# Output bias written by ScalarE under an accumulating gather of the residual, in a sparse graph-attention kernel

## The chip, the cores and the metric

The kernel runs on one core of a Trainium2 chip, in one launch. The metric is the device time of that launch in microseconds (us). Three runs of the kernel before gave 1980.19, 1983.63 and 1985.25 us; the median, 1983.63 us, is the time before. The profiled execution took 1980.11 us and its span, from the first to the last instruction, is 1978.3 us.

## The reference

A layer of graph attention with a residual and a layer norm, for x of 16 x 1024 x 512 and one 1024 x 1024 adjacency matrix of zeros and ones (few ones: a node has a handful of neighbours, a few nodes have many), all float32:

```python
q = (x @ Wq + bq).reshape(b, n, H, HD)      # H = 8 heads of HD = 64
k = (x @ Wk + bk).reshape(b, n, H, HD)
v = (x @ Wv + bv).reshape(b, n, H, HD)
scores = einsum('bqhd,bkhd->bhqk', q, k) / sqrt(HD)
scores = scores + (1.0 - adj)[None, None, :, :] * -1000000000.0
attn = softmax(scores, axis=-1)
out = einsum('bhqk,bkhd->bqhd', attn, v).reshape(b, n, d)
attn_out = out @ Wo + bo
x = _layernorm(x + attn_out, axis=-1)       # mean and variance over the 512, eps 1e-5
```

The change concerns the last two lines alone: the output product, its bias (`bo`), the residual x and the sum over the 512 columns that the layer norm starts from. The kernel folds the value bias through Wo into the output bias once, at the start (L345), so that `bo_bc`, a 128 x 512 tile, holds the whole bias, the same in every partition.

## The kernel before

**Tiling.** A batch is 1024 nodes, taken as 8 tiles of 128 queries. At the start the kernel counts the neighbours of each node, sorts the nodes by that count and writes lists of neighbours; `asked_row` holds, for each tile, the rows of its 128 queries in x. The attention of a tile is done in blocks, each with one neighbour per query: 35 blocks per batch, 560 in all. For a block, GpSimd gathers the key and value rows (`kvg`, L849), VectorE multiplies and sums (`qk` L870, `s` L874), ScalarE takes the exponential (L884) and weighs the value rows, eight small instructions per block (L894; for some blocks VectorE does it, L898), and VectorE adds up (L910); for the nodes with many neighbours TensorE adds up (`sum`, L919 and L920). `normalise` then divides (o, L939), TensorE transposes o (`poT`, L947) and ScalarE copies the transposed tile out of PSUM (`oT`, L951).

**Fronts.** The products of x with the query, key and value weights of all batches are a list of units, `fronts`, worked off between the blocks (L565 for the query, L679 for key and value, which are done by a scheme with fewer products and more additions). The last fronts are placed some blocks before the last batch begins.

**Finishing a tile.** `finish` (L760) makes the output product of a transposed tile (`po`, four matmuls of 128x512, L565) and plans what follows: `out` adds the product to the residual tile `y`, with the row sum as a by-product (`accum_out`), then `centre`, `spread` (ScalarE squares, L781), `variance`, `power` (GpSimd, L787), `shift`, `norm_out` (ScalarE, L793) and `store`, a scatter by GpSimd into the output (L797). The bias enters in one of two ways. While there are fronts left, VectorE makes two passes, `y = p + y` (L771) and `y = bo_bc + y` with the row sum (L772). When no fronts are left (`biased`), TensorE adds the bias by a fifth matmul of 128x512 in the middle of the output product (L814), and VectorE makes one pass (L772 with p in place of bo_bc).

**The residual tile.** `load_y` (L743) takes a buffer of the tag "y" (6 of them) and fills it ahead of the finishing: for the tiles 0 to 101 by an indirect gather of 128 rows of x (`gather_x`, L732, GpSimd), for the tiles 102 to 127 by a plain load by SyncE of a tile that was sorted at the start. That sorting is `sort_residual` (L738): two tiles a step over 13 steps of the start, each a gather into a "y" buffer and, two steps later, a store by SyncE to DRAM (`residual`). So the y gathers are 26 at the start and 102 in the course of the work. The tiles 102 to 111 also have their transposed attention output spilled to DRAM and reloaded when the fronts are done, so that the finishing of the last 22 tiles or so falls into the last stage.

**What sets the order.** The order on each engine is written out by the program: one pass of the main loop (L1045) is a step, about one block. Within a step come the exponentials of block n + 3, the products of n + 4, the gathers up to n + 8, the weighing, the sums, then what was planned for this step by `later(k, fn)` (k steps ahead), then `later_last`, then the loads of y for tiles that will be finished soon, and then units of TensorE (finishing first, fronts after) as far as a credit goes. `sort_residual` is called at the end of a step. Each engine works through its own list in that order, and waits on semaphores where it needs another engine or a transfer. A tile is finished two steps after its y was asked for at the earliest (`n > loaded + 1`), and its `out` comes a step after its last matmul.

Of the kernel before, what the change touches and what calls it, by code (L numbers as in the profile page):

```python
# [14 lines left out]
OP = mybir.AluOpType  # L15
# [33 lines left out]
PRODUCT = 0.86  # L49
# [6 lines left out]
P = 128  # L56
# [103 lines left out]
def kernel(  # L160
# [36 lines left out]
    nc = tc.nc  # L197
# [15 lines left out]
    ident = const.tile([P, P], F32, name="ident")  # L213
    make_identity(nc, ident)
    W = {}
# [3 lines left out]
    bo_bc = const.tile([P, D], F32, name="bo_bc")  # L219
# [8 lines left out]
    with ExitStack() as main:  # L228
# [6 lines left out]
        def fill_psum(name):  # L235
            return psum.tile([P, HALF], F32, tag="fill", name=name, bufs=4)
# [48 lines left out]
        residual = [dram.tile([P, D], F32, name=f"residual_{i}") for i in range(B * NT - SPILL[0])]  # L285
# [65 lines left out]
        def later(k, fn):  # L351
            plan.setdefault(now[0] + k, []).append(fn)

        def later_last(k, fn):
            rest.setdefault(now[0] + k, []).append(fn)
# [167 lines left out]
        X, XT, SX, KV, VSUM, NRM, Y, OT, PS = {}, {}, {}, {}, {}, {}, {}, {}, {}  # L523
# [35 lines left out]
        def product(name, lhs, w, out):  # L559

            def unit(c):
                if c == 0:
                    PS[name] = fill_psum(name)
                p = PS[name]
                nc.tensor.matmul(p, lhs()[:, ts(c, P)], w[:, c, :], start=(c == 0), stop=(c == NPAIR - 1))  # L565
                if c == NPAIR - 1:
                    del PS[name]
                    later(1, lambda: out(p))

            return [(PRODUCT, lambda c=c: unit(c), None) for c in range(NPAIR)]  # L570
# [159 lines left out]
        loaded = {}  # L730

        def gather_x(y, b, t):  # L732
            nc.gpsimd.indirect_dma_start(  # L733
                out=y, out_offset=None, in_=x_rows,
                in_offset=bass.IndirectOffsetOnAxis(ap=asked_row[:, t:t + 1], axis=0), element_offset=b * N * D,
            )

        def sort_residual(i):  # L738
            y = work.tile([P, D], F32, tag="y", name=f"y_sorted_{i}", bufs=Y_BUFS)
            gather_x(y, *divmod(SPILL[0] + i, NT))  # L740
            later(2, lambda: nc.sync.dma_start(residual[i], y))

        def load_y(b, t, k=None):  # L743
            if k is None:
                Y[b, t] = work.tile([P, D], F32, tag="y", name=f"y_{b}_{t}", bufs=Y_BUFS)
            else:
                Y[b, t] = work.tile([P, 2, D], F32, tag=f"t{k % 4 + 1}", name=f"y_{b}_{t}", bufs=1)[:, 0, :]
            loaded[b, t] = now[0]
            if b * NT + t >= SPILL[0]:
                nc.sync.dma_start(Y[b, t], residual[b * NT + t - SPILL[0]])  # L750
            else:
                gather_x(Y[b, t], b, t)
# [6 lines left out]

        def finish(b, t):  # L760


            biased = not fronts

            def out(p):
                OT.pop((b, t))
                y = Y[b, t]

                st = small.tile([P, 5], F32, name="stats", bufs=6)
                if not biased:  # L770
                    nc.vector.tensor_tensor(y, p, y, op=OP.add)  # L771
                nc.vector.scalar_tensor_tensor(  # L772
                    y, p if biased else bo_bc, 1.0, y, op0=OP.mult, op1=OP.add, accum_out=st[:, 0:1]
                )

                def centre():
                    nc.vector.tensor_scalar(st[:, 1:2], st[:, 0:1], -1.0 / D, None, op0=OP.mult)

                def spread():
                    sq = work.tile([P, D], F32, tag="ysq", name=f"ysq_{b}_{t}", bufs=1)  # L780
                    nc.scalar.activation(sq, y, AF.Square, bias=st[:, 1:2], accum_out=st[:, 2:3])  # L781

                def variance():
                    nc.vector.tensor_scalar(st[:, 2:3], st[:, 2:3], 1.0 / D, EPS, op0=OP.mult, op1=OP.add)  # L784

                def power():
                    nc.gpsimd.tensor_tensor(st[:, 3:4], st[:, 2:3], neg_half, op=OP.pow)  # L787

                def shift():
                    nc.vector.tensor_tensor(st[:, 4:5], st[:, 3:4], st[:, 1:2], op=OP.mult)  # L790

                def norm_out():
                    nc.scalar.activation(y, y, AF.Identity, bias=st[:, 4:5], scale=st[:, 3:4])  # L793
                    later(2, store)

                def store():
                    nc.gpsimd.indirect_dma_start(  # L797
                        out=out_rows[b, t], out_offset=bass.IndirectOffsetOnAxis(ap=asked_row[:, t:t + 1], axis=0),
                        in_=y, in_offset=None, element_offset=b * N * D,
                    )  # L800
                    del Y[b, t]

                later(1, centre)
                later_last(2, spread)
                later(3, variance)
                later(4, power)
                k = 5 if fronts else 6
                later(k, shift)
                later_last(k + 1, norm_out)

            units = product(f"po_{b}_{t}", lambda: OT[b, t], W["o"], out)
            if biased:
                def bias():
                    nc.tensor.matmul(  # L814
                        PS[f"po_{b}_{t}"], ident[:, 0:1].to_broadcast([P, P]), bo_bc, start=False, stop=False
                    )

                units.insert(2, (PRODUCT, bias, None))
            return units

# [198 lines left out]
        done, coming, spilled, gathered, fronts, guarded = [], [], [], [0], [], []  # L1021
# [9 lines left out]
        with tc.manual_schedule():  # L1031
# [13 lines left out]
            while n < total or plan or rest or urgent or done or finishing or spilled or not guarded:  # L1045
# [45 lines left out]
                while credit > 0 or urgent:  # L1091
                    if urgent and not (first_unit and fronts):
                        urgent.pop(0)()
                        continue
                    if (
                        not finishing and len(done) > (LAZY if fronts else 0) and n > loaded.get(done[0], n) + 1
                        and n > last_finish + 1 and not total - 2 <= n < total
                    ):
                        finishing = finish(*done.pop(0))
                        last_finish = n  # L1100
                    units = finishing or fronts
                    if not units:
                        if urgent:
                            urgent.pop(0)()
                            continue
                        break
                    cost, fn, ready = units[0]
                    if ready and not ready():
                        if urgent:
                            urgent.pop(0)()  # L1110
                            continue
                        break
                    del units[0]
                    fn()
                    credit -= cost
                    first_unit = False
# [3 lines left out]
                if n in SORTED_AT:  # L1120
                    for i in range(2):
                        sort_residual(2 * (n - SORTED_AT[0]) + i)
# [35 lines left out]
```

## Time and profile before

| | |
|---|---|
| time, median of three runs | 1983.63 us |
| span of the profile | 1978.3 us |
| granted TensorE clock, mean | 0.990 |
| moved by the DMA engines | 563.10 MB, 285 GB/s in the mean |
| of it by GpSimd's queue | 403.22 MB, 61.4% of 16 engines' time |
| of it by SyncE's queue | 153.16 MB, 20.9% |
| gathers of y (102 and 26), 256 KB each | median 5.1 and 6.4 us from issue to landing |
| gathers of key and value rows (560), 512 KB each | median 5.9 us |
| scatters of the output (128), 256 KB each | median 5.2 us |
| finished tiles with the bias on VectorE, on TensorE | 106, 22 |

How to read it: the span is one execution; the busy time of an engine is the time in which it had an instruction in work. A row of a group of instructions gives the line, the engine, the operation, the tiles (out<-in), the count, then the busy time in us and the mean in ns of one; after the bar stands how long the engine was idle just before such instructions, and what it waited for. TensorE's float32 matmul is recorded as two instructions, so 22 bias products stand there as x44. A mean duration overlaps with the next instruction's; where a cost is wanted, the distance from start to start in the time line is the better number.

### The profile page before, as it was taken

The numbers are of one execution on the slowest core, as the hardware profiler recorded it, in microseconds if no ns is written. First come the engines' busy times: TensorE is split into PE (matmuls) and PEld (weight loads), VectorE is DVE, ScalarE is ACT, GpSimd is POOL, SyncE is SP. The second block draws the span as 40 slices with busy tenths as digits, with TensorE's granted clock in tenths as the row PEclk, the third lists the DMA queues.
The fourth block names the chain that finished last, engine by engine and source line by source line (L and its number), as shares of the span: only waits on it lengthen the run. The fifth ranks groups of instructions, "written<-read, shape, count | busy, mean of one in ns | idle before, by whom it ended". The sixth has DMA issues, their size and how long they took to land. (4 is left out here: it accounts for less than half of the span.)

```text
span 1978.3 us, 25784 instructions
## 1 busy us (share of the span) xinstructions
PE 1913.1 (97%) x5379; PEld 925.0 (47%) x5379; DVE 1785.8 (90%) x3694; ACT 1566.4 (79%) x6152; POOL 1301.4 (66%) x1224
## 2 busy tenths in 40 slices
PE   7988999999999999999999999999999999899896
PEld 4434454444545454454545445454544545444443
DVE  3799999998999999999998999999899999999785
ACT  4526788888787888879887887979888798988895
POOL 1663566767667675767667686766767675566784
PEclk9999999999999999999999999999999999999898
DMA  6796887888889788888879788888978889988984
GB/s 252 219 366 244 263 303 247 301 284 279 303 272 323 262 305 270 303 287 286 304 260 319 257 301 277 295 304 267 315 254 288 285 311 311 321 308 287 317 290 143
DMA packets 191140, 563.10 MB, mean 285 GB/s; under 512 B 31711, under 2 KB 31739, under 8 KB 190974
## 3 DMA queue, kind: packets, MB, share of 16 engines
q0 software_dynamic: 121632, 403.22, 61.4%
q1 hardware_dynamic: 66736, 153.16, 20.9%
q10 hardware_dynamic: 2606, 4.99, 0.7%
q14 instruction: 122, 1.00, 0.2%
q8 instruction: 44, 0.72, 0.1%
HBM read 442.25 MB, written 143.71 MB: 296 GB/s over the span
## 5 line engine op out<-in xcount | busy, mean ns | idle before, releaser
L849 POOL DMA_INDIRECT kvg<-kv_rows,key_row x560 | 632.7, 1130 | 425.3 <-ACT pv L894 123.1
L894 ACT ACTIVATE pv<-kvg,pv 128x64 f32<-128x64 f32 x3608 | 908.7, 339 | 0.1
L565 PE MATMUL pq<-wq,xT 128*128 128x512 f32 x1024 | 477.4, 596 | 1.5 <-DVE q L595 0.9
L565 PE MATMUL po<-wo,oT 128*128 128x512 f32 x944 | 437.0, 595 | 4.7 <-DVE y L771 1.9
L874 DVE TENSOR_REDUCE s<-qk 128x8 f32<-128x512 f32 x560 | 381.1, 681 | 6.1
L870 DVE TENSOR_TENSOR qk<-qt,kvg 128x512 f32<-128x512 f32 x464 | 317.6, 684 | 3.6 <-DMA kvg<-kv_rows,key_row 3.6
L565 PEld LDWEIGHTS pq<-wq,xT 128*128 128x128 f32 x1024 | 191.4, 191 | 219.8 <-issue 201.6
L565 PEld LDWEIGHTS po<-wo,oT 128*128 128x128 f32 x944 | 175.4, 191 | 206.0 <-issue 189.4
L679 PE MATMUL pp<-t,s 128*128 128x512 f32 x504 | 237.2, 593 | 6.3 <-DVE s L551 6.3
L679 PE MATMUL x<-b,xT 128*128 128x512 f32 x504 | 237.1, 593 | 0.0
L910 DVE TENSOR_TENSOR pv<-pv,pv 128x520 f32<-128x520 f32 x336 | 233.3, 694 | 0.0
L884 ACT ACTIVATE pv<-s,absent 128x8 f32<-128x8 f32 x464 | 135.8, 293 | 105.8 <-DVE s L874 67.8
L797 POOL DMA_INDIRECT out_dram<-y,asked_row x128 | 152.4, 1190 | 38.9 <-issue 21.0
L833 POOL DMA_INDIRECT qt<-q_rows,asked_row x128 | 140.9, 1101 | 36.7 <-issue 33.1
L575 ACT ACTIVATE sq_k<-kv 128x128 f32<-128x128 f32 x512 | 150.7, 299 | 8.8 <-DVE kv L702 8.8
L679 PEld LDWEIGHTS pp<-t,s 128*128 128x128 f32 x504 | 94.7, 190 | 115.3 <-issue 103.4
L679 PEld LDWEIGHTS x<-b,xT 128*128 128x128 f32 x504 | 94.7, 190 | 112.2 <-issue 107.6
L733 POOL DMA_INDIRECT y<-in_x_dram,asked_row x102 | 117.2, 1149 | 30.6 <-issue 28.5
L843 POOL DMA_INDIRECT qg<-q_rows,query_row x96 | 105.9, 1103 | 26.8 <-issue 23.0
L679 PE MATMUL z<-t,s 128*128 128x512 f32 x252 | 120.2, 600 | 0.0
L679 PE MATMUL z<-b,s 128*128 128x512 f32 x252 | 118.6, 593 | 1.2 <-DVE kv L707 1.2
L679 PE MATMUL pp<-t,xT 128*128 128x512 f32 x252 | 118.4, 592 | 0.0
(185 smaller groups left out, 2625.7 us busy)
## 6 DMA issues: line engine op xcount, KB each, us to landing
kv_rows<-kv SPq DMA_DIRECT2D x128, 512.0 KB
x<-in_x_dram SPq DMA_DIRECT2D x128, 256.0 KB
q_rows<-q SPq DMA_DIRECT2D x128, 256.0 KB
kvg<-kv_rows,key_row POOLq DMA_INDIRECT x560, 5.9
residual<-y_sorted SPq DMA_DIRECT2D x26, 256.0 KB
y<-residual SPq DMA_DIRECT2D x26, 256.0 KB
adj<-in_adj_dram POOLq DMA_DIRECT2D x8, 512.0 KB, 10.9
spill<-oT SPq DMA_DIRECT2D x10, 256.0 KB
```

The lines of the kernel that those rows point to most:

```text
L565: nc.tensor.matmul(p, lhs()[:, ts(c, P)], w[:, c, :], start=(c == 0), stop=(c == NPAIR - 1))
L575: nc.scalar.activation(sq, s[:, ts(h, P)], AF.Square, scale=scale, accum_out=sums[:, h:h + 1])
L679: nc.tensor.matmul(R[bank], l[:, ts(c, P)], right[:, c, :], start=(first and c == 0), stop=(c == 1), skip_group_check=True,)
L733: nc.gpsimd.indirect_dma_start(out=y, out_offset=None, in_=x_rows, in_offset=bass.IndirectOffsetOnAxis(ap=asked_row[:, t:t + 1], axis=0), ...
L797: nc.gpsimd.indirect_dma_start(out=out_rows[b, t], out_offset=bass.IndirectOffsetOnAxis(ap=asked_row[:, t:t + 1], axis=0), in_=y, in_offse ...
L833: nc.gpsimd.indirect_dma_start(out=QT[b, t], out_offset=None, in_=q_rows[b % ROWS], in_offset=bass.IndirectOffsetOnAxis(ap=asked_row[:, t: ...
L849: nc.gpsimd.indirect_dma_start(out=KG[n], out_offset=None, in_=kv_rows[b % ROWS], in_offset=bass.IndirectOffsetOnAxis(ap=key_row[:, g:g + ...
L870: nc.vector.tensor_tensor(QK[n], q, KG[n][:, 0:D], op=OP.mult)
L874: nc.vector.tensor_reduce(S[n], QK.pop(n).rearrange("p (h d) -> p h d", d=HD), axis=AX.X, op=OP.add)
L884: nc.scalar.activation(PV[n][:, D:], S.pop(n), AF.Exp, bias=bias)
L894: nc.scalar.activation(pv[:, ts(h, HD)], v[:, ds(D + h * HD, HD)], AF.Copy, scale=pv[:, D + h:D + h + 1])
L910: nc.vector.tensor_tensor(PV[b, t], PV[b, t], pv, op=OP.add)
```

## The change

The bias is taken out of `finish` altogether. Before the gather of a y tile, ScalarE copies `bo_bc` into the tile, and one step later GpSimd gathers the rows of x with an addition (`compute_op=OP.add`), so that the DMA engines add x to the bias that is there. `y` then holds x + bias when it is used, VectorE needs one pass in every tile, and TensorE no bias matmul in any. In the sorting at the start the store to DRAM moves from two steps after the call to three, since the gather is issued one step later. The aim is to take the bias off VectorE and TensorE.

```diff
         def gather_x(y, b, t):
-            nc.gpsimd.indirect_dma_start(
+
+            nc.scalar.copy(y, bo_bc)
+            later(1, lambda: nc.gpsimd.indirect_dma_start(
                 out=y, out_offset=None, in_=x_rows,
                 in_offset=bass.IndirectOffsetOnAxis(ap=asked_row[:, t:t + 1], axis=0), element_offset=b * N * D,
-            )
+                compute_op=OP.add,
+            ))
 
         def sort_residual(i):
             y = work.tile([P, D], F32, tag="y", name=f"y_sorted_{i}", bufs=Y_BUFS)
             gather_x(y, *divmod(SPILL[0] + i, NT))
-            later(2, lambda: nc.sync.dma_start(residual[i], y))
+            later(3, lambda: nc.sync.dma_start(residual[i], y))
...
         def finish(b, t):
 
-
-            biased = not fronts
-
             def out(p):
                 OT.pop((b, t))
                 y = Y[b, t]
 
                 st = small.tile([P, 5], F32, name="stats", bufs=6)
-                if not biased:
-                    nc.vector.tensor_tensor(y, p, y, op=OP.add)
-                nc.vector.scalar_tensor_tensor(
-                    y, p if biased else bo_bc, 1.0, y, op0=OP.mult, op1=OP.add, accum_out=st[:, 0:1]
-                )
+                nc.vector.scalar_tensor_tensor(y, p, 1.0, y, op0=OP.mult, op1=OP.add, accum_out=st[:, 0:1])
...
-            units = product(f"po_{b}_{t}", lambda: OT[b, t], W["o"], out)
-            if biased:
-                def bias():
-                    nc.tensor.matmul(
-                        PS[f"po_{b}_{t}"], ident[:, 0:1].to_broadcast([P, P]), bo_bc, start=False, stop=False
-                    )
-
-                units.insert(2, (PRODUCT, bias, None))
-            return units
+            return product(f"po_{b}_{t}", lambda: OT[b, t], W["o"], out)
```

## The prediction

> **What bounds the kernel now.** First the page's line of busy times, for the engine that is nearest to full. Then the busy times by stretch, because the kernel has stages: columns are the stretch, its length, the busy us (and instructions) of TensorE's matmuls, weight loads, VectorE, ScalarE and GpSimd, the granted clock, the DMA engines' share and GB/s. The first row below is the start, in which the 26 residual tiles are sorted; the others are the bulk and the end.
>
> ```profile
> PE 1913.1 (97%) x5379; PEld 925.0 (47%) x5379; DVE 1785.8 (90%) x3694; ACT 1566.4 (79%) x6152; POOL 1301.4 (66%) x1224
> ```
>
> ```profile
> 75.00:155.00 80.00, 71.53 (x183) 31.61 (x182) 72.96 (x139) 22.71 (x91) 51.35 (x48) 1.00 0.95 344
> 210.00:1650.00 1440.00, 1436.04 (x4067) 696.74 (x4066) 1345.10 (x2753) 1194.30 (x4756) 998.10 (x918) 1.00 0.85 288
> 1770.00:1831.00 61.00, 59.11 (x157) 27.69 (x158) 56.80 (x118) 54.16 (x218) 37.89 (x36) 1.00 0.85 286
> 1831.00:1862.00 31.00, 31.00 (x85) 15.09 (x84) 25.42 (x61) 23.64 (x91) 21.33 (x23) 1.00 0.95 339
> 1862.00:1931.00 69.00, 56.33 (x147) 25.68 (x145) 59.11 (x153) 64.14 (x235) 56.54 (x61) 0.92 0.85 288
> 1931.00:1963.00 32.00, 30.07 (x79) 15.25 (x79) 21.81 (x67) 22.56 (x73) 19.40 (x22) 0.91 0.54 180
> ```
>
> The reader is to see three regimes. From 210 to 1650 us TensorE is idle for 4 us in 1440: it alone sets the pace, and VectorE (93%) and ScalarE (83%) have room. From 1831 to 1862 TensorE is still full. From 1862 to 1931 it is not (82%); ScalarE is the fullest (93%), and VectorE is at 86%.
>
> Then the groups that the change touches (busy us, mean ns | idle before):
>
> ```profile
> L814 PE MATMUL po<-bo_bc,ident 128*128 128x512 f32 x44 | 23.4, 615 | 0.0
> L772 DVE SCALAR_TENSOR_TENSOR y<-bo_bc,y 128x512 f32<-128x512 f32 x106 | 73.6, 695 | 3.7
> L771 DVE TENSOR_TENSOR y<-po,y 128x512 f32<-128x512 f32 x106 | 72.4, 683 | 8.3 <-PE po L565 8.1
> L733 POOL DMA_INDIRECT y<-in_x_dram,asked_row x102 | 117.2, 1149 | 30.6 <-issue 28.5
> L951 ACT COPY oT<-poT 128x512 f32<-128x512 f32 x128 | 73.7, 576 | 46.1 <-PE po L565 35.3 <-PE poT L947 10.7
> ```
>
> Last the waits. This is who waited for whom from 1862 us on, of TensorE and of VectorE:
>
> ```profile
> PE poT L947 <- DVE o L939: 7.4, 4, 2.8
> PE poT L947 <- DVE stats L777: 3.7, 1, 3.7
> ...
> DVE y L772 <- PE po L565: 8.9, 3, 3.5
> DVE stats L790 <- POOL stats L787: 8.1, 8, 2.8
> ```
>
> After 1862 TensorE waits for VectorE (11.1 us) and VectorE waits for TensorE (8.9 us) and for the statistics chain through GpSimd (8.1 us): a coupled tail, in which no single engine's time comes off in full.
>
> **What the Trainium skill says.** (1) "ScalarE: Activation LUTs", section "What ACT_TABLE_LOAD costs": an activation with immediate scale and bias takes 186 ns + 0.833 ns per column, successive ones overlap by about 93 ns. At 512 columns that is 612 ns, 519 from start to start, an estimate from this page. The trace has no such copy from SBUF; copies from PSUM take 576 ns and follow each other after 0.47 us, so it agrees to a tenth. (2) "DMA: Bandwidth & Descriptors", section "SDMA does more than copy": an addition in the DMA engine reduces two streams; section "Rules for kernel authors": it reads its destination and writes it later. So a gather of 256 KB reads 512 KB. No rate is given, and no transfer of before adds. (3) "TensorE: Matmul & The Clock Gate", Part 1: about 3.4 us of idleness halve the clock. The trace agrees: after the gaps at 1865 to 1871 us two output products take 3.78 us in place of 1.88, and the clock of 1862 to 1931 is 0.92.
>
> **The change part by part.**
>
> TensorE loses 22 bias products. In the time line the next product begins 0.86 us after each (1832.81, 1833.67), so 22 x 0.86 = 18.9 us, all after 1831. The order of the remaining TensorE work is unchanged. By stretch: 6 products (5.2 us) lie in 1831 to 1862, where TensorE is full. Squeezed to 25.8 us that stretch would have VectorE, with 25.4 us of work, at 98%, so I count **4 us**. 14 products (12.0 us) lie between 1862 and 1950. There ScalarE is fullest, and TensorE's wait for its last sums at 1949 us ends on VectorE. What comes back is the time in which VectorE really waited for a product held up by a bias: 3.0 us at 1877, of which the bias is 1.4 (it ran at the low clock). I count **1.5 us**. The last 2 products, at 1954.3 and 1960.4, stand in the closing chain (product, y, statistics, store), with nothing beside it: **1.7 us**. Sum 7.2 us.
>
> VectorE loses the pass L771, 106 times. Start to start such passes are 0.60 us apart, so 64 us. About 100 of these lie in 210 to 1650, where TensorE idles only 4 us in all: at most 1 us comes back, hidden by TensorE's full list. None lies between 1621 and 1771. Six lie in 1771 to 1820, where VectorE is 93% busy and TensorE lost 1.9 us in one wait for y L771: **1 us** of that. The remaining pass of L772 reads PSUM and was 688 ns in the 22 tiles that had that form already, so it costs nothing new. Together 2 us.
>
> ScalarE gains 128 copies, between 0.47 us (trace) and 0.61 us (page, no overlap); I take 0.52: 66 us. About 100 in the bulk make its share 1246 of 1440, 87%, hidden under TensorE. None is in the last stage, since tiles from 102 on come from the sorted copies. A copy lengthens the way of a PSUM tile by 0.5 us when it is queued ahead of L951, L600 or L692, which TensorE's four-deep PSUM ring covers. At the start ScalarE is busy 22.7 us of 80, but there a copy waits until the store of the tile six before has landed, which is now issued in the same step as the copy. Queued behind it are the PSUM copies L692, L600 and L540, for which VectorE and then TensorE wait. They themselves now wait 3 to 10 us for TensorE at each step, so most of such a stall is hidden: 0 to 5 us, I take **2 us lost**.
>
> GpSimd: the gathers move one step later and wait for the copy. Queued behind are the kvg gathers, but the next of them waits for ScalarE's weighing in that same step anyway, and kvg is fetched eight steps ahead: nothing. Descriptors for two streams might lengthen 1149 ns by as much again, 128 x 1.15 = 147 us on an engine at 66%: hidden. The y gathers were issued 10 us or more (mostly 12 to 15) before VectorE used y. One step later, about 3.2 us, leaves 7 us or more for a landing that took 5.2 (at most 8.2): a few waits, inside VectorE's room.
>
> DMA: GpSimd's queue took 61.4% of the span for 403 MB, so 256 KB cost 0.79 us of all engines. From below an addition costs nothing more; if double, 0.79 us more. I take double and keep triple as the other end. In the bulk that is 102 x 0.79 = 81 us, from a share of 0.85 to 0.90: hidden. At the start it is 26 x 0.79 = 20.6 us in a stretch with 4 us free. Some 17 us spill past 155 us, where the kvg gathers issued at 146 us and landed 6 us later are first used at 171.5: 19 us of slack. Just hidden.
>
> Sum: 7.2 + 2 - 2 = 7.2 us; from 1983.6 it gives **1976.4 us**.
>
> **The rivals.** *All of TensorE's time comes back*: the busy 97% and the 8.9 us that VectorE waits for po speak for it, ScalarE's 93% after 1862 against. 1983.6 - 18.9 - 2 = 1962.7 us. *The tail absorbs it*: earlier TensorE work only idles longer, and the low clock costs some of it again; only the closing 1.7 us remains and the start takes it back: 1983.6 us. For it speaks that VectorE and ScalarE are each over 85% there, against it the full 1831 to 1862. *The adding gather is dear*: at triple cost 41 us come on top at the start, 18 more than the slack and the free 4 us hold, and ScalarE stalls 5 us behind the stores: 18 + 5 - 9 = 14 us slower, 1998 us. The share of 0.95 there speaks for it; that the sorted tiles are needed only 1600 us later, against.
>
> **How the numbers follow.** Forecast 0.45, all back 0.17, absorbed 0.13, dear 0.25. The bound of 0.3% is 6 us. The forecast lies 1.2 us beyond it and its terms carry some 3 us each way, so about 0.31 of its 0.45 is faster, 0.14 same; all back is faster. The absorbed case gives 0.10 same, 0.02 faster, 0.01 slower; dear is slower but for 0.02 same. Faster 0.50, same 0.26, slower 0.24. Range 1962 to 1994: it leaves out a little of all back and half of dear.
>
> **What would show it.** L814 and L771 gone, L772 128 times at about 690 ns, copies of some 0.5 to 0.6 us on ScalarE. The fronts should end near 1831 as before, give or take 3 us; 1831 to 1862 shorter by 4 us; the closing chain by 1.7. VectorE should fall to 87%, ScalarE rise to 83%, the DMA share by some 5 points. It would be wrong if the step at which the bulk begins (near 200 us) moved by over 5 us, if TensorE between 210 and 1650 idled over 10 us, waiting for y or kvg, or if landing of the y gathers went beyond 9 us.

## The result, and the profile after

The changed kernel takes **1998.77 us** (median of four runs, 1997.04 to 2000.43) against 1984.44 us of the kernel before on the same chip: ratio **1.0075, interval 1.0056 to 1.0094**. It is slower; forecast were 1976.4 us. The profiled executions span 1978.3 us before and 1998.7 us after, 20.4 us apart; TensorE's idle time grew by 28.1 us (span less busy: 65.2 to 93.3), while its busy time fell by only 7.7, though the 22 bias products are gone. What is left of it takes longer, in part at a lower clock: the mean granted clock fell from 0.990 to 0.987, about 6 us of the span (an estimate from these two).

First the page after: busy times, GpSimd's DMA queue, the gathers of the key and value rows and of y. The groups' columns are busy us, mean ns of one, then the idle time just before them and what ended most of it.

```profile
PE 1905.4 (95%) x5335; PEld 918.3 (46%) x5335; DVE 1716.6 (86%) x3588; ACT 1630.4 (82%) x6280; POOL 1375.4 (69%) x1224
...
q0 software_dynamic: 129824, 403.22, 65.4%
...
L837 POOL DMA_INDIRECT kvg<-kv_rows,key_row x560 | 638.1, 1139 | 288.2 <-issue 85.4
...
L735 POOL DMA_INDIRECT y<-in_x_dram,asked_row x102 | 172.3, 1689 | 129.3 <-ACT pv L872 112.1
```

The gather of y took 1149 ns before, with 30.6 us of idle time in front of all 102; now it takes 1689 ns and has 129.3 us in front of it. The new and the changed rows on ScalarE and VectorE, from the groups by line:

```profile
L734 ACT COPY y<-bo_bc 128x512 f32<-128x512 f32 x102 | 62.2, 610 | 0.0
L734 ACT COPY y_sorted<-bo_bc 128x512 f32<-128x512 f32 x26 | 15.2, 615 | 33.4 <-DMA residual<-y_sorted 33.4
...
L770 DVE SCALAR_TENSOR_TENSOR y<-po,y 128x512 f32<-128x512 f32 x128 | 87.7, 685 | 32.7 <-DMA y<-in_x_dram,asked_row 16.6 <-PE po L565 15.4 <-PE pq L565 0.7
L786 DVE TENSOR_TENSOR stats<-stats 128x1 f32<-128x1 f32 x128 | 19.7, 154 | 74.6 <-POOL stats L783 74.6
```

The passes and copies are as forecast. The last row is not: L786 is `shift`, which waits for the power step of GpSimd (L783). These are the waits that changed most (us in all, times, longest), first the two of them that the kernel before had, in its own line numbers, then all five after:

```profile
DVE stats L790 <- POOL stats L787: 20.2, 18, 2.9
...
DVE qk L870 <- DMA kvg<-kv_rows,key_row: 3.6, 4, 1.7
```

```profile
POOL y L735 <- ACT pv L872: 112.1, 53, 5.8
DVE stats L786 <- POOL stats L783: 74.6, 46, 4.2
ACT y_sorted L734 <- DMA residual<-y_sorted: 33.4, 13, 6.5
DVE qk L858 <- DMA kvg<-kv_rows,key_row: 19.8, 16, 3.3
DVE y L770 <- DMA y<-in_x_dram,asked_row: 16.6, 12, 2.8
```

The first, third and fifth did not exist before. The first names the ScalarE instruction after the copy (L872), but it is the copy that is waited for: of the 47 of these 102 gathers that stood for over 0.5 us, 45 begin 0.27 to 0.29 us after the copy's end, three of them while L872 is still running.

Where the time goes is told by stretches. The columns are the stretch, its length, busy us and instructions of TensorE's matmuls, weight loads, VectorE, ScalarE and GpSimd, the granted clock, the DMA share and GB/s. First before, then after:

```profile
100.00:200.00 100.00, 87.77 (x243) 41.56 (x242) 96.63 (x213) 46.91 (x197) 50.95 (x46) 0.97 0.83 303
...
330.00:860.00 530.00, 528.08 (x1495) 256.46 (x1494) 496.19 (x1021) 441.60 (x1756) 376.56 (x347) 1.00 0.85 291
860.00:1650.00 790.00, 790.00 (x2241) 383.66 (x2240) 741.74 (x1519) 659.36 (x2624) 550.09 (x505) 1.00 0.85 288
```

```profile
100.00:200.00 100.00, 82.58 (x230) 38.71 (x229) 90.66 (x200) 50.45 (x187) 59.71 (x45) 0.93 0.98 305
...
330.00:860.00 530.00, 519.16 (x1454) 249.60 (x1453) 460.34 (x962) 453.58 (x1760) 385.35 (x336) 0.99 0.88 282
860.00:1650.00 790.00, 788.88 (x2234) 382.82 (x2233) 703.03 (x1461) 680.38 (x2656) 577.00 (x502) 1.00 0.89 286
```

TensorE loses 5 us of work at the start (100 to 200), where its clock is lower too (0.93 for 0.97), and from 330 to 860 it idles 10.8 us in place of 1.9; from 860 to 1650 it is full before and idles 1.1 us after. An event that occurs once a batch, ScalarE's copy `mean`, gives the delay of after against before along the way: +5.0 us at 214 us, +9.7 at 571, +18.4 at 802, +20.7 at 1629, +21.6 at 1837 and +20.4 at the end. So in this pair of executions the tail, from which 7.2 us were hoped, gave 1.2, and the loss came mostly at the start and before 860.

One occurrence in the time line of after (start, duration, engine, line; in brackets the idle time before and its releaser; other rows left out):

```profile
788.46 0.60 ACT L734 COPY y<-bo_bc 128x512 f32<-128x512 f32 x1
...
788.96 0.30 ACT L872 ACTIVATE pv<-s,absent 128x8 f32<-128x8 f32 x1
...
789.33 1.56 POOL L735 DMA_INDIRECT y<-in_x_dram,asked_row  x1 [5.46 <-ACT pv L872]
...
791.19 1.00 POOL L821 DMA_INDIRECT qt<-q_rows,asked_row  x1 [0.30 <-issue]
...
792.50 1.44 POOL L837 DMA_INDIRECT kvg<-kv_rows,key_row  x1 [0.30 <-issue]
...
793.96 0.58 POOL L783 TENSOR_TENSOR stats<-stats,neg_half 128x1 f32<-128x1 f32 x1
...
794.58 0.16 DVE L786 TENSOR_TENSOR stats<-stats 128x1 f32<-128x1 f32 x1 [0.93 <-POOL stats L783]
```

GpSimd stands 5.46 us until the copy ends at 789.06, begins 0.27 us later, needs 1.56 us, and then works off what had piled up: two gathers with 0.30 us between them, and only then the tiny power step, for which VectorE already waits. No rows of GpSimd's own work show the loss; it is the order of its queue.

How such a lateness reaches TensorE is seen some 30 us earlier. From 742 to 766 us GpSimd works off its queue with no pause over 0.31 us. VectorE waits 2.21 us for the power step at 750 us and 0.57 us for kvg at 760, and is then so late with emptying TensorE's PSUM tile (q, L595) that TensorE waits for it. The last row is the stretch from 762 to 769 us, with its granted clock of 0.52:

```profile
763.37 1.11 PE L536 MATMUL pxT<-ident,x 128*128 128x128 f32 x4 [2.58 <-DVE q L595]
764.28 3.62 PE L679 MATMUL z<-t,s 128*128 128x512 f32 x4
...
762.00:769.00 7.00, 5.63 (x10) 2.83 (x11) 4.76 (x8) 6.52 (x28) 4.76 (x5) 0.52 0.92 330
```

The product after the wait takes 3.62 us, where the same four take 1.88 elsewhere. The wait (2.6 us) and the slow clock (0.48 of 7 us, 3.4) come to about 6 us, an estimate from these rows: most of the 6.6 us by which the delay grew from 688 us (11.8) to 802 us (18.4). So one wait of TensorE, with the slow clock that set in during it, cost more than twice its own length. The kernel that has the change in the bulk alone (below) has the same wait, 2.50 us, and a clock of 0.89 from 755 to 770 us; before, and without any bias, TensorE is full there at 1.00.

### The profile page after: what moved, and what is told of

It is laid out like the page before. It is cut to its first block, busy times and chain, and to the rows that moved or that the text cites. A ratio compares the mean times of both kernels' runs of the same rounds, so it can differ in the third digit from the quotient of the medians.

```text
span 1998.7 us, 25741 instructions
## 1 busy us (share of the span) xinstructions
PE 1905.4 (95%) x5335; PEld 918.3 (46%) x5335; DVE 1716.6 (86%) x3588; ACT 1630.4 (82%) x6280; POOL 1375.4 (69%) x1224
## 3 DMA queue, kind: packets, MB, share of 16 engines
q0 software_dynamic: 129824, 403.22, 65.4%
q1 hardware_dynamic: 66736, 153.16, 20.7%
## 5 line engine op out<-in xcount | busy, mean ns | idle before, releaser
L735 POOL DMA_INDIRECT y<-in_x_dram,asked_row x102 | 172.3, 1689 | 129.3 <-ACT pv L872 112.1
L872 ACT ACTIVATE pv<-s,absent 128x8 f32<-128x8 f32 x464 | 137.2, 296 | 112.3 <-DVE s L862 57.3
L821 POOL DMA_INDIRECT qt<-q_rows,asked_row x128 | 148.2, 1158 | 37.3 <-issue 31.0
L793 POOL DMA_INDIRECT out_dram<-y,asked_row x128 | 144.1, 1126 | 39.8 <-issue 22.3
L679 PEld LDWEIGHTS x<-b,xT 128*128 128x128 f32 x504 | 94.8, 190 | 112.1 <-issue 108.0
```

The lines of the kernel that those rows point to most:

```text
L679: nc.tensor.matmul(R[bank], l[:, ts(c, P)], right[:, c, :], start=(first and c == 0), stop=(c == 1), skip_group_check=True,)
L735: later(1, lambda: nc.gpsimd.indirect_dma_start(out=y, out_offset=None, in_=x_rows, in_offset=bass.IndirectOffsetOnAxis(ap=asked_row[:, t: ...
L793: nc.gpsimd.indirect_dma_start(out=out_rows[b, t], out_offset=bass.IndirectOffsetOnAxis(ap=asked_row[:, t:t + 1], axis=0), in_=y, in_offse ...
L821: nc.gpsimd.indirect_dma_start(out=QT[b, t], out_offset=None, in_=q_rows[b % ROWS], in_offset=bass.IndirectOffsetOnAxis(ap=asked_row[:, t: ...
L872: nc.scalar.activation(PV[n][:, D:], S.pop(n), AF.Exp, bias=bias)
```

## The experiments

All ratios are to the kernel before on the same chip, with 95% intervals. Where the course along the way is compared, it is one execution of each kernel, and single executions of one kernel differ by some us. Theory of the queue: GpSimd stands at the y gather for ScalarE's copy, its gather is longer, and what is behind it (the power step, the kvg gathers) comes late. Rivals: ScalarE's added work, the doubled reading of the DMA engines, the one step that y comes later, the sorting at the start.

### Parts taken out one by one

**No bias at all**, the gather and the stores at the start as before: what the removals are worth.

```diff
-            nc.scalar.copy(y, bo_bc)
-            later(1, lambda: nc.gpsimd.indirect_dma_start(
+            nc.gpsimd.indirect_dma_start(
...
-                compute_op=OP.add,
-            ))
+            )
```

> The changed kernel without any bias: no copy on ScalarE, no addition in the gather, the gather of y issued at once as in the kernel before, stores of the sorted tiles two steps later as before. It leaves the output bias out. So only the removals of the change are left: 106 VectorE passes and 22 TensorE products. By the prediction's own sum the removals are worth 9.2 us, which gives 1975 us against 1984.4 of before. If all of TensorE's 18.9 us came back: 1964 us. If the tail absorbs the removal: 1982 to 1984 us. The 14 us that the change lost must then lie in what it adds.

Measured 1977.32 us, **0.9965 (0.9953 to 0.9977)**. Its profile spans 3.6 us less than before, but it is already 6.1 us ahead at 571 us and 4.4 ahead at 1837 us: in this pair the gain comes early, and TensorE's 22 products return nothing. Who TensorE waits for from 1837 us on shows why; first before, then without bias:

```profile
PE poT L947 <- DVE o L939: 7.4, 4, 2.8
PE poT L947 <- DVE stats L777: 3.7, 1, 3.7
...
PE sum L919 <- DVE stats L784: 0.7, 1, 0.7
```

```profile
PE poT L932 <- DVE o L924: 12.4, 4, 5.5
PE sum L904 <- DVE pv L883: 5.3, 4, 1.9
PE poT L932 <- DVE stats L770: 5.3, 2, 4.6
```

TensorE is 16.5 us less busy there (111.5 to 95.0). Its own waits, with the smaller rows, rise from 14.5 to 27.6 us, nearly all of the rise for VectorE.

One pair does not settle it. The stretch from that mark to the end takes 141.5 us before and 142.3 without bias. In the traces of all runs, but for three in which tiles are finished late, it takes 137.5 to 143.4 us in the 13 without these products (mean 140.7) and 141.5 to 145.8 in the four with them (mean 143.5, two of the four on a slower chip). So the products may be worth some 3 us, an estimate from these means, but not their 18.9. Nor is the early lead shown to be VectorE's: the control further below, the kernel before with a later shift, keeps both passes and stands 3.8 us ahead at 571 us in its trace, with no gain in its time.

**Copy kept, gather without addition** (the line `compute_op=OP.add` taken out):

> The changed kernel with the copy on ScalarE and the gather one step later, but the gather overwrites in place of adding (the bias is copied and then lost: it leaves the output bias out). Queue theory: the loss comes from GpSimd standing at the y gather until ScalarE has copied, with the power step and the kvg gathers behind it, and from ScalarE standing at the copy until a store has landed; then this stays near the changed kernel, 1993 to 1999 us, with VectorE waiting some 60 to 75 us for the power step. Addition theory: the loss comes from the addition in the transfer (1.6 in place of 1.0 us on GpSimd, 0.72 us of all DMA engines per gather); then this is near the kernel without bias, 1975 to 1984 us.

Measured 1983.73 us, **0.9993 (0.9983 to 1.0003)**: 0.0028 over no bias, some 5.5 us. GpSimd stands even longer at y (142.8 us), yet the wait for the power step is 45.1 us and not 74.6: the stand alone does not make the loss.

**Addition kept, no copy**, onto six fixed tiles that are cleared once (two tiles of the set-up that shared the tag move to another):

```diff
+        ring = [work.tile([P, D], F32, tag=f"y{i}", name=f"y_{i}", bufs=1) for i in range(Y_BUFS)]
+        for y in ring:
+            nc.gpsimd.memset(y, 0.0)
...
-            nc.scalar.copy(y, bo_bc)
```

> The changed kernel with the adding gather, one step later, but without the copy on ScalarE: the gather adds to what the tile last held, so the output is x plus left-over content (the bias is left out). The six y tiles are cleared once at the start and taken in turn. Queue theory: with nothing to wait for on ScalarE the loss is gone, 1975 to 1984 us, and VectorE waits some 20 us for the power step as before. Addition theory: 1993 to 1999 us.

Measured 1982.29 us, **0.9988 (0.9979 to 0.9996)**: 0.0023 over no bias. Gathers of 1604 ns (median), power wait 32.5 us: the addition alone does not make it either.

**Neither, but the gather one step later** (both lines taken out, `later(1, ...)` kept):

> The changed kernel with neither copy nor addition: a plain gather of y, but one step later, and the later stores (it leaves the output bias out). Both theories: near the kernel without bias, 1975 to 1984 us. If it is 5 us or more slower than that one, the lateness of y, VectorE waiting for its landing, is a cause of its own.

Measured 1976.77 us, **0.9959 (0.9945 to 0.9973)**: the step of lateness alone costs nothing.

So the copy costs 0.0028, the addition 0.0023, and both together 0.0110 (1.0075 less 0.9965), twice their sum. Each run fell where the other theory had put it, so a theory of one cost that simply adds up was dead here.

**ScalarE's work alone**: the copies go to a tile that nobody waits for, and the gather is plain and at once.

```diff
-            nc.scalar.copy(y, bo_bc)
+            nc.scalar.copy(work.tile([P, D], F32, tag="ysq", name=f"aside_{b}_{t}", bufs=1), bo_bc)
```

> The kernel without bias (plain gather of y at once) with the 128 copies of the bias tile on ScalarE in their places, but into a tile that nobody waits for (it leaves the output bias out). ScalarE's load without the wait at GpSimd. If the wait is the cost of the copy: 1977 to 1979 us, as without copies. If ScalarE's load is: 1983 to 1985 us, as with the copy under the plain gather.

Measured 1981.69 us, **0.9978 (0.9967 to 0.9989)**: 0.0013 over no bias, 2.6 us, which is within the two intervals. ScalarE's load is at most a small part.

**Start alone and bulk alone**: the copy with the adding gather only in the sorting, and then only in the 102 others; the rest is gathered plainly, without bias.

> Copy and adding gather for the 26 tiles sorted at the start alone; the 102 gathers of the bulk are plain, at once, with no bias (it leaves the output bias out of the tiles 0 to 101). From the marks of the work at 214 us in the profiles (5.0 us late in the changed kernel, 1.5 us early with the late plain gather) the start should cost 6 us: 1983 us. If the loss of the start is made up later: 1977 to 1979 us.

> Copy and adding gather for the 102 tiles of the bulk alone; the 26 tiles of the start are gathered plainly, at once, and stored two steps later as before (it leaves the output bias out of the tiles 102 to 127). By the difference: 1999 less the 6 us of the start, 1991 to 1994 us. If the bulk loses only because the start has eaten its lead: 1980 to 1985 us.

Start alone 1988.17 us, **0.9999 (0.9985 to 1.0014)**, and bulk alone 1998.58 us, **1.0058 (1.0042 to 1.0073)**: 0.0034 and 0.0093 over no bias, 6.7 and 18.4 us. They add up to about the whole loss over no bias (0.0127 against 0.0110, within the intervals), so they are nearly independent. At the start ScalarE stands 32.7 us for the stores of the sorted tiles, and from 75 to 155 us the DMA share is 0.99, where no bias has 0.96.

### What in the bulk

**Gather two steps after the copy**, so that GpSimd need not stand (`later(1, ...)` to `later(2, ...)` in the bulk):

> The changed kernel, with the adding gather of the 102 tiles in the bulk issued two steps after the copy in place of one (the sorting at the start is as in the changed kernel). ScalarE has then copied before GpSimd comes to the gather. Queue theory (GpSimd standing at the y gather holds back the power step and kvg): GpSimd's wait at the y gather falls from over 110 us to under 20, VectorE's wait for the power step from 75 to about 35 us (what the kernel with the addition alone showed), and the time falls by some 5 to 9 us to about 1990 to 1994. Rival (ScalarE's 66 us of copies are the cost, the wait only shows it): no change, 1997 to 2000 us, or slower, since y lands later and VectorE waits for it.

Measured 2005.82 us, **1.009 (1.0076 to 1.0105)**, not faster: a miss. The waits tell why:

```profile
DVE y L770 <- DMA y<-in_x_dram,asked_row: 49.3, 27, 3.4
DVE stats L786 <- POOL stats L783: 42.3, 24, 3.6
...
POOL y L735 <- ACT pv L872: 7.2, 16, 0.8
```

GpSimd's stand fell from 112.1 to 7.2 us and the power wait from 74.6 to 42.3, as the theory has it, but y is now late: 49.3 us of waits in place of 16.6. One wait was traded for another.

**y asked for one tile earlier**, and then **the same with the gather two steps after the copy**. The bookkeeping (`asked_at`) is meant to keep the finishing where it was; the second run has the later gather of the run above besides:

```diff
                 for tile_done in done[:0 if fronts and len(done) < LAZY else 1 if fronts else 2] + coming:
+                    asked_at.setdefault(tile_done, n)
+                for tile_done in done[:2] + coming:
...
-                        not finishing and len(done) > (LAZY if fronts else 0) and n > loaded.get(done[0], n) + 1
+                        not finishing and len(done) > (LAZY if fronts else 0) and n > asked_at.get(done[0], n) + 1
```

> The changed kernel, with y asked for one tile (some 4 blocks, 13 us) earlier, copy and gather both; the tiles are finished where they were. GpSimd still comes to the gather a step after the copy. If y's late landing is the cost (copy, then a gather that takes longer to issue and to land): VectorE's wait for y falls from 17 us to nothing and the ratio from 1.0075 to 1.002 to 1.004. If the cost is what stands behind the gather on GpSimd: no change, 1.006 to 1.009.

> Both: y asked for one tile earlier and the gather two steps after the copy, so that GpSimd neither stands at the gather nor is y late. If the two waits together are the loss of the bulk: it costs what the addition and ScalarE's copies cost by themselves, some 5 us each above the kernel without bias with the 6 us of the start, a ratio of 1.001 to 1.004. If the loss is in the load itself (ScalarE's copies and GpSimd's longer gathers in the same stretches): 1.006 to 1.009.

Measured **1.0107 (1.009 to 1.0124)** and **1.0054 (1.0041 to 1.0068)**. These two have to be compared with each other: the bookkeeping forgot the ten reloaded tiles, which both finish up to two steps later in the last stage than the changed kernel does (see the mended version). Between them only the gather's step differs, and 0.0053, 10.5 us, come back, with GpSimd's stand at 8.8 us (108.2) and the power wait at 41.0 (76.4). In the first no wait for y's landing is left, and it is no faster. Its late finishing weighs on that, but at 1837 us, ahead of it, its trace is still 17.7 us behind before (the changed kernel's 21.6), so late y is at most a small part of the loss.

**Shift one step later**, so that VectorE reaches it when the power step is done (`k = 6` in place of `k = 5 if fronts else 6`), in the changed kernel and, as a control, in the kernel before:

> The changed kernel, with the step after the power (shift, the first VectorE instruction that needs GpSimd's power) one step later while there are fronts; all else in its order. If VectorE's 75 us of waiting for a power step that stands behind the y gather on GpSimd is the cost: the wait falls to some 20 us and the time by 6 to 12 us (ratio to before 1.001 to 1.004 in place of 1.0075). If these waits fall into VectorE's spare time: no change, 1.006 to 1.009.

> The kernel before with its shift step one step later while there are fronts (nothing else changed), the control for the same edit in the changed kernel, which gained 6 us there. If that gain was the mending of a wait that the change made, this does nothing here (VectorE waits only 20 us for the power step): ratio 0.999 to 1.001. If a later shift is better in any case, it gains here as well: 0.997.

Measured 1990.72 us, **1.0044 (1.0029 to 1.0059)**, so 6 us of the changed kernel's loss come back with that wait (74.6 to 21.0 us), though VectorE's waits for late kvg rise from 19.8 to 31.3 us. The kernel before with it: 1983.39 us, **1.0003 (0.9997 to 1.001)**, nothing.

### GpSimd's time or the DMA engines'

The addition makes GpSimd's gather 0.54 us longer in the mean and takes more of the DMA engines' time. Memsets after each y gather give the first without the second.

```diff
+                for _ in range(6):
+                    nc.gpsimd.memset(idle, 0.0)
-                compute_op=OP.add,
```

> The kernel with the copy and a plain overwriting gather (ratio 0.9993), with six small memsets on GpSimd after each y gather, some 0.6 us in all: the time that the addition costs on GpSimd without its transfer (it leaves the output bias out). If the addition works through GpSimd's time: near the changed kernel, 1.004 to 1.0075. If it works through the DMA engines and the landing: 0.999 to 1.001.

Six memsets (0.93 us) with the copy: 2024.55 us, **1.0214 (1.0197 to 1.0231)**, power wait 115.6 us. With the stand, GpSimd's time is enough to make a loss, but the dose was too large. So three memsets (0.45 us, where the expectation reckoned 0.6), with the copy and without it:

> The changed kernel without its addition (the output lacks the bias), but with three small memsets by GpSimd after each gather of y, of about 0.6 us together, which is what the addition makes such a gather longer. The copy by ScalarE, and GpSimd's wait for it, stay. If GpSimd's time and its wait are what the bulk costs, and not the doubled reading of the DMA engines, this comes near the changed kernel: ratio to before 1.005 to 1.009, with VectorE waiting 60 to 90 us for the power step. If it is the addition in the DMA engines (late or crowded transfers), it stays near the kernel with the copy and no addition: 0.999 to 1.001.

> The same three memsets after each gather of y, without copy and without addition (the output lacks the bias): GpSimd's time alone, with no wait for ScalarE. If the loss needs both, the longer gather and the wait for the copy, this lies with the kernel that adds without the copy, ratio 0.998 to 1.000. If GpSimd's time alone is enough, it comes to 1.004 or more, and the wait for the copy matters little.

With the copy 1998.38 us, **1.0077 (1.0062 to 1.0091)**; without it 1980.4 us, **0.9988 (0.998 to 0.9996)**. The ratios as a square, with nothing of the bias beside them:

| | gather waits for nothing | gather waits for the copy |
|---|---|---|
| plain gather | 0.9965 (one step later: 0.9959) | 0.9993 |
| gather with addition | 0.9988 | 1.0075 (the changed kernel) |
| plain gather and 0.45 us of memsets | 0.9988 | 1.0077 |

The last two rows agree in both columns, far closer than their intervals. The waits follow; first the memsets with the copy, then without:

```profile
POOL y L738 <- ACT pv L878: 106.9, 54, 5.6
...
DVE stats L792 <- POOL stats L789: 83.4, 50, 4.8
```

```profile
DVE stats L791 <- POOL stats L788: 35.4, 26, 3.3
```

The excess over the sum needs both, the stand and the longer work, and the addition's transfer is not needed for it. One reservation: that the totals agree so well is in part luck. From 214 to 1837 us the memsets lose 16.4 us and the changed kernel 16.6, but at 214 us they stand at +1.6 and +5.0, the tail makes up the difference, and of the 16.4 us 5.4 come between 1629 and 1837. So for the start a share of the DMA engines is not excluded.

### A mended version

All of the reference is computed: sorting as before, the bias of those 26 tiles as before, for the others the copy and the adding gather, with y asked for earlier (the bookkeeping above), the gather two steps after the copy and the shift one later.

```diff
-            gather_x(y, *divmod(SPILL[0] + i, NT))
-            later(3, lambda: nc.sync.dma_start(residual[i], y))
+            plain_x(y, *divmod(SPILL[0] + i, NT))
+            later(2, lambda: nc.sync.dma_start(residual[i], y))
...
-                gather_x(Y[b, t], b, t)
+                gather_x(Y[b, t], b, t, 2)
...
-                k = 5 if fronts else 6
+                k = 6
```

> A mended version that computes all of the reference: the 26 residual tiles of the start are sorted without bias as in the kernel before, and their tiles get the bias as before (TensorE, or a second pass of VectorE while there are fronts). The other 102 have the copy and the adding gather, but y is asked for one tile earlier, the gather comes two steps after the copy so that GpSimd doesn't stand, and the shift is one step later. By the sums of the single runs: 1.0058 for the bulk alone, less 0.0053 for the gather that need not wait and 0.003 for the shift gives 0.9975 (0.996 to 0.9995), a little faster than before. If the queue of GpSimd isn't the cause, it stays at 1.003 to 1.006; if the tail's bias on TensorE costs its 19 us after all, 1.005 or more.

Measured 1991.98 us, **1.0043 (1.003 to 1.0056)**: a miss. In its trace the bulk from 214 to 1837 us loses 5.2 us against before (the changed kernel 16.6), so the mending works there, if not in full, and the tail loses 7.7. In the tail TensorE's order was not that of before, since the reloaded tiles were finished late. With that put right by one line (`asked_at[b, t] = now[0]` after the reload's `load_y`), and once with SyncE writing the bias tile in place of ScalarE:

> The mended version once more, with one thing put right: asking for y earlier had also put off the finishing of the ten reloaded tiles in the last stage by up to two steps, so that TensorE's order there was not that of before; now its whole order is that of the kernel before. The mended version stood 4.2 us behind before at the last mark before the tail (1837 us) and 11.9 us at the end, so 7.7 us came in the tail. If the late finishing made them, this gives 1.0043 less 0.0039, 1.0004 (0.999 to 1.002); if they come from the bulk (a changed state of the queues on entering the tail), it stays at 1.003 or more.

> The same, but the bias is put into the y tile by a DMA from SyncE instead of ScalarE's copy. ScalarE's copies alone cost 0.0013 (2.6 us), so if only engines count this is faster than the run beside it by that: 0.999 (0.9975 to 1.0005). But 256 KB more are moved per tile, about 0.8 us of all DMA engines each, in a bulk whose share is 0.85 to 0.90; and GpSimd now waits for a transfer in place of a copy. If that wait lasts beyond the two steps, GpSimd stands again and it is slower than the run beside it, 1.003 to 1.007.

Measured 1992.72 us, **0.9993 (0.9975 to 1.0011)**, and 2000.45 us, **1.003 (1.0016 to 1.0045)**. These two ran on a chip where the kernel before takes 1995.10 us, so their times are compared with that alone; why it is slower there is not known, and no trace of before was taken on it. The waits of the first:

```profile
DVE stats L799 <- POOL stats L796: 7.6, 9, 1.6
POOL y L741 <- ACT pv L893: 7.1, 14, 0.8
```

and of the second:

```profile
POOL y L741 <- DMA y<-bo_bc: 58.9, 20, 5.1
DVE qk L879 <- DMA kvg<-kv_rows,key_row: 34.1, 25, 4.2
```

With the stand and the power wait gone the slowdown is gone; the edits came together, so what each did is not told apart here. With a transfer in place of the copy GpSimd stands again, for the transfer, and a part of the slowdown is back. The power wait is not (3.8 us); what grew is VectorE's waiting for kvg, from 14.4 to 34.1 us. The 256 KB more that are moved per tile remain a rival for that: the DMA share from 210 to 1650 us is 0.93 for 0.89. A version that is faster than the kernel before was not found: 0.9993 can't be told from 1.

## Why the prediction was wrong

**TensorE, 7.2 us in the tail: fell.** The three terms (4 + 1.5 + 1.7) were read from busy shares in three stretches. Without any bias the tail returned nothing (4.4 us ahead at 1837, 3.6 at the end), in the changed kernel 1.2 us, and in the mean of all traces some 3. The rival "the tail absorbs it" came nearer: TensorE's own wait for VectorE took the place of the products. One reading of a trace in the prediction is too wide: the slow products of 1870.88 us follow gaps of 2.76, 1.49 and 1.64 us, so they show the halved pace (3.78 for 1.88 us), but not one stretch of idleness as long as the prediction names for it.

**VectorE, 2 us: perhaps too small.** The removals together are worth 6.9 us (0.9965), near the 9.2 that the prediction had for them. In the traces the lead comes before 600 us, where only VectorE's passes are gone, but the control with both passes has a lead of 3.8 us there as well. So how the 6.9 us divide between VectorE and TensorE is not shown. (From 1771 to 1820 us VectorE is 96% busy, 47.16 of 49 us; the prediction's 93% is that of the longer row.)

**ScalarE: right in size, but the start was not.** 66 us were forecast, and its busy time rose by 64.0 (1566.4 to 1630.4); one copy takes 610 to 615 ns, against the 612 ns that the prediction estimated from the Trainium skill's page "ScalarE: Activation LUTs", section "What ACT_TABLE_LOAD costs". The next instruction begins 0.50 us after the copy's start (788.46, 788.96), where the same estimate had 519 ns. As mere load it costs at most some 2.6 us where nothing was counted. The stall at the start was put at 2 us and the DMA spill at nothing; the start cost 6.7, with the DMA engines at 0.99 there.

**GpSimd, "147 us on an engine at 66%: hidden": the step that failed.** The longer gather was thought of at 1.15 us, and measured 0.54. The size was no problem; the word "hidden" was, and with it the "nothing" for the wait on the copy. Of the queue behind the gather, only the kvg gathers were named, and held to be safe; VectorE's waits for them rose from 3.6 to 19.8 us. The power step stands there too, and VectorE's next statistics wait for it (20.2 to 74.6 us). And 66% is the share of busy time in an engine that leaves 0.30 us between one gather and the next: counting pauses of up to 0.31 us, GpSimd's fullest 80 us of the bulk are full to 98% already before, and to 100% after. In place of nothing, the bulk cost 18.4 us over no bias, of which a later shift alone returns 6.

**y one step later: right**, "a few waits": 12 waits, 16.6 us, and the lateness alone costs nothing.

**DMA engines: right in size.** q0's time rose from 61.4% of 1978.3 to 65.4% of 1998.7 us, 92.5 us, or 0.72 us for each of 128 gathers, against 0.79 forecast for a double reading. In the bulk this was hidden, as forecast: nearly the same loss comes without it (16.4 and 16.6 us).

**The rival at 1998 us** hit the number, not the cause. It had 18 us of DMA spill and 5 us of stall at the start; the added time was that of a double reading, not a triple one, the start cost 6.7 us, and the bulk, which it left out, 18.4.

Two of the prediction's signs of being wrong came, if barely: TensorE idled 12.9 us between 210 and 1650 (4.0 before), though nearly all of it for VectorE and not for y or kvg directly, and the longest landing of a y gather was 9.1 us in the bulk and 9.3 at the start. The mark at 214 us was 5.0 us late.

What is not settled: how the 18.4 us of the bulk divide after the 6 us of the power step. One late instruction with the slow clock after it is some 6 us of it in the trace. Late kvg gathers are one part by their waits (19.8 us in the changed kernel, 5.7 without bias), but no run took out their lateness alone. Nor was tried why TensorE idles from 330 to 860 and no longer from 860 on.

## What to carry to other kernels

When an instruction gets a new wait, list everything behind it in its engine's queue, small instructions too, and ask who waits for each; the price of the wait is paid there. A stand and a longer instruction that each cost some 5 us alone cost twice their sum here when they came together: test such a pair as a square. For an engine that issues gathers, read how closely they follow in the time line, not the busy share. And before the course of two traces is laid to a cause, look at the same stretch in the traces of the other runs.

## What the runs showed of the hardware

- An indirect gather of 256 KB with an addition keeps GpSimd busy for 1598 ns, a plain one for 988 (medians). The Trainium skill, "DMA: Bandwidth & Descriptors", section "SWDGE vs HWDGE vs iDMA", has GpSimd compute such descriptors in software; the longer instruction agrees with that. The queue's packets rose by 8192, 64 for each of 128 gathers, with the same bytes counted.
- Two gathers in a row on GpSimd start 1.24 us apart at best: about 0.95 us and a gap of 0.30 us that the profile calls "issue" (1.31 us from 791.19 to 792.50 above).
- The landing of y grew from a median of 5.1 to 5.8 us in the bulk, and from 6.4 to 7.8 at the start.
